# Second MLP product of a token tower from seven products of quarters

## The chip, the cores and the metric

The kernel runs on one core of one Trainium2 chip. The metric is the device time of one execution in microseconds; the time before is the median of three runs. A core has a matrix engine (TensorE, PE in the profile; PEld is its loading of weights), three engines for element-wise work (VectorE or DVE, ScalarE or ACT, GpSimd or POOL), an engine that here issues transfers (SyncE, SP), a working memory SBUF of 128 partitions, and the accumulator memory PSUM into which TensorE writes.

## The reference

A signal of shape (4, 64, 512, 64) is cut into patches, Fourier transformed and multiplied by a weight matrix: 16,384 tokens of 256 numbers. One layer follows: a retention block with an MLP, and a mixture of 8 experts of which each token takes 2. All in fp32. Cut to what matters here:

```python
# h: tokens [16384, 256]; x = layernorm(h)
hh = layernorm(x)
q, k, v = hh @ Wq.T + bq, hh @ Wk.T + bk, hh @ Wv.T + bv
mem_t = decay * mem_(t-1) + k_t * v_t          # scan along 4096 tokens
x = x + q * mem
h2 = layernorm(x)
mlp = relu(h2 @ W1.T + b1) @ W2.T + b2         # 256 -> 1024 -> 256
h = h + (x + mlp)
t = layernorm(h)                                # router and experts work on t
h = h + t + sum over two experts e of share_e * (gelu(t @ w1[e] + b1[e]) @ w2[e] + b2[e])
```

The change concerns the second product of the MLP, `relu(...) @ W2.T`: per block of 512 tokens a matrix of 512x1024 by one of 1024x256.

## The kernel before

32 blocks of 512 tokens (4 tiles of 128) go through a pipeline. In each period of the loop one block (`new`) is embedded, normalised and goes through retention, the block before it (`mid`) through the MLP, and the one before that (`old`) is routed: its rows are written to lists, one per expert, from which expert tiles of 256 rows are then taken. One such tile is worked off in a `slot`: `enter` (first expert product), `leave` (second product of the tile before), `sums` (results of that tile). The order of instructions on TensorE, VectorE and ACT is the order of the program text. The numbers D, KD, KH, TT, U are 256, 2, 8, 4 and 2.

```python
class Norm:
    def stats(self, src, t): ...              # bn_stats and bn_aggr on VectorE
    def factors_here(self): ...               # 1/sqrt(var + eps) on VectorE, 12 small operations
    def factors(self, twice=False): ...       # the same by pow on GpSimd
    def apply(self, dst, src, i=0):
        for t in range(TT):
            nc.vector.tensor_scalar(
                dst[:, t, :D], src[:, t, :], self.mv[:, t, 0:1],
                self.rstd[:, i, t : t + 1], ALU.subtract, ALU.mult)
...
    def residual(self):                       # block `new`, after retention
        norm = Norm()
        for u in range(U):
            ps = p_tm.tile([P, 2, D], F32, name="tm")
            for i in range(2):
                for k in range(KD):
                    nc.tensor.transpose(ps[:, i, ts(k, P)],
                        self.ret[:, k, ts(2 * u + i, P)], ident)
            nc.vector.tensor_tensor(self.z[:, ts(u, 2), :], ps, self.z[:, ts(u, 2), :], ALU.add)
            for i in range(2):
                norm.stats(self.z, 2 * u + i)
        norm.factors_here()
        self.zz = one.tile([P, TT, D], F32, name="zz")
        norm.apply(self.zz, self.z)
...
    def mlp_in(self, m):                      # aT: features x tokens, after the Relu
        ps = feature_mm(w1_sb, self.hT, m)    # two matmuls with 512 moving columns
        nc.scalar.activation(self.aT[:, m, :], ps, AF.Relu, bias=vec[:, MB1 + m : MB1 + m + 1])

    def mlp_out(self, u, between=None):
        if u == 0:
            self.norm = Norm()
        ps = p_tm.tile([P, 2, D], F32, name="tm")
        for i in range(2):
            ...
            for k in range(KH):
                nc.tensor.matmul(ps[:, i, :], lhsT=self.aT[:, k, ts(u * 2 + i, P)],
                    rhs=w2_sb[:, k, :], start=k == 0, stop=k == KH - 1)
        nc.vector.tensor_tensor(self.h[:, ts(u, 2), :], ps, self.h[:, ts(u, 2), :], ALU.add)
        for i in range(2):
            self.norm.stats(self.h, u * 2 + i)
        if u == U - 1:
            ...factors...
            self.tok = one.tile([P, TT, D], F32, name="tok")
            self.norm.apply(self.tok, self.h)
            ...
```

A period of the loop, with the engines that do most of each step:

```python
            next(embed)                # 40 matmul records of 256 columns, then stats, factors, apply
            ...
            slot(known)
            for m in range(KH):
                if mid: mid.mlp_in(m)
                if m == 1: new.split1()            # ACT; then a transposing DMA
                if m == TT - 1: slot(known)
                if m == KH - 3:
                    blocks[i + 1].differences(xs.pop(i + 1))
                    new.features1()                # hT from the DMA's result
            if old: ...logits...                   # router product
            for m in range(KD):
                new.retention(m)                   # 6 matmuls of 512 columns; kv, scan, ret on VectorE
                if old and m == 0: old.choose()
            if old: take(old.i + 1, old, old.place())
            slot(known)
            if mid: mid.mlp_out(0)
            new.residual()
            slot(known)
            ...
            new.split2()
            if mid: mid.mlp_out(1)
```

PSUM has three pools here: `p_mm` with four buffers, `p_tm` with three, `p_sm` with one[...].

Of the kernel before, what the change touches and what calls it, by code (L numbers as in the profile page):

```python
# [12 lines left out]
F32 = mybir.dt.float32  # L13
# [6 lines left out]
P = 128  # L20
# [15 lines left out]
def vit_tower_kernel(  # L36
# [20 lines left out]
    E = rw.shape[1]  # L57
    KD, KH = D // P, H // P
    J = STRIDE // 2
    TT = 4  # L60
# [88 lines left out]
    nc.sync.dma_start(out=w1_sb, in_=w1.rearrange("(k p) h -> p k h", p=P))  # L149
    w2_sb = const.tile([P, KH, D], F32)  # L150
    nc.sync.dma_start(out=w2_sb, in_=w2.rearrange("(k p) d -> p k d", p=P))
    rw_sb = const.tile([P, KD, E], F32)
# [62 lines left out]
    class Norm:  # L215
# [23 lines left out]
        def factors(self, twice=False):  # L239

            n = 2 if twice else 1
            self.rstd = small.tile([P, n, TT], F32, name=f"rstd{n}")
            nc.gpsimd.tensor_scalar(self.rstd[:, 0, :], self.mv[:, :, 1], EPS, None, ALU.add)  # L243
            if twice:
                nc.gpsimd.tensor_scalar(
                    self.rstd[:, 1, :], self.mv[:, :, 1], 1.0 + EPS, EPS * EPS, ALU.mult, ALU.add
                )
            nc.gpsimd.tensor_tensor(self.rstd, self.rstd, mhalf[:, 0:n, :], ALU.pow)

        def apply(self, dst, src, i=0):  # L250
# [58 lines left out]
    class Block:  # L309
# [32 lines left out]
        def embed(self):  # L342
# [38 lines left out]
            norm.factors(twice=True)  # L381
            yield
            self.z = one.tile([P, TT, D], F32, name="z")
            self.zz = one.tile([P, TT, D], F32, name="zz")
            norm.apply(self.zz, self.h, 1)
            norm.apply(self.z, self.h, 0)

# [57 lines left out]
        def residual(self):  # L445
            norm = Norm()
            for u in range(U):
# [7 lines left out]
                for i in range(2):  # L455
                    norm.stats(self.z, 2 * u + i)
            norm.factors_here()
            self.zz = one.tile([P, TT, D], F32, name="zz")
            norm.apply(self.zz, self.z)

# [4 lines left out]
        def split2(self):  # L465
            if self.i < EARLY:
                return
            self.turn = Turn()
            self.turn.split(self.zz)
# [8 lines left out]
        def mlp_in(self, m):  # L478
# [3 lines left out]
            nc.scalar.activation(self.aT[:, m, :], ps, AF.Relu, bias=vec[:, MB1 + m : MB1 + m + 1])  # L482

        def mlp_out(self, u, between=None):
            if u == 0:
                self.norm = Norm()
            ps = p_tm.tile([P, 2, D], F32, name="tm")
            for i in range(2):
                if i and between:
                    between()  # L490
                for k in range(KH):
                    nc.tensor.matmul(  # L492
                        ps[:, i, :],
                        lhsT=self.aT[:, k, ts(u * 2 + i, P)],
                        rhs=w2_sb[:, k, :],
                        start=k == 0,
                        stop=k == KH - 1,
                    )
            nc.vector.tensor_tensor(self.h[:, ts(u, 2), :], ps, self.h[:, ts(u, 2), :], ALU.add)
            for i in range(2):  # L500
                self.norm.stats(self.h, u * 2 + i)
            if u == U - 1:
                self.norm.factors_here() if self.i >= NS - 1 else self.norm.factors()
                self.tok = one.tile([P, TT, D], F32, name="tok")
                self.norm.apply(self.tok, self.h)
                if self.i == NS:
                    nc.vector.tensor_tensor(self.h, self.h, self.tok, ALU.add)
                    return
                mean, rstd = self.norm.mv[:, :, 0], self.norm.rstd[:, 0, :]
                self.by = small.tile([P, 2, TT], F32, name="by")  # L510
                nc.vector.tensor_scalar(self.by[:, 0, :], rstd, 1.0, None, ALU.add)
                nc.vector.scalar_tensor_tensor(self.by[:, 1, :], mean, -1.0, rstd, ALU.mult, ALU.mult)

        def store(self):

            by = self.by
            for t in range(TT):
                nc.scalar.activation(  # L518
                    self.h[:, t, :],
                    self.h[:, t, :],  # L520
                    AF.Identity,
                    bias=by[:, 1, t : t + 1],
                    scale=by[:, 0, t : t + 1],
                )

            self.stored = nc.sync.dma_start(out=rows_of(self.i), in_=self.h)
            unordered("sums", self.stored, ())

        def rows(self):

            self.row = two.tile([P, TT, RW], I32, name="row")
            for i, half in enumerate(halves(self.tok)):
# [154 lines left out]
    def take(n, block, writes):  # L687
# [24 lines left out]
        shape = [1, k, E]  # L712
        past = small.tile([1, KMAX, E], F32, name="past")[:, :k, :]
        nc.vector.tensor_tensor(
# [4 lines left out]
        )  # L719
        table_f = small.tile([1, 2, KMAX], F32, name="table_f")[:, :, :k]  # L720
        nc.vector.tensor_reduce(table_f[:, 0, :], past, AX.X, ALU.add)
# [214 lines left out]
    LEFT = 3  # L936

    def slot(known):

# [9 lines left out]
    with tc.manual_schedule(engines=MANUAL):  # L949
        blocks[0].differences(xs.pop(0))  # L950
        xs[1] = load_x(1)
        for i in range(NS):
# [14 lines left out]
            next(embed)  # L967
            next(embed)
            if mid:
                mid.sum_up()  # L970
            next(embed, None)
            slot(known)
# [4 lines left out]
            for m in range(KH):  # L977
                if mid:
                    mid.mlp_in(m)
                if m == 1:  # L980
                    new.split1()
                if m == TT - 1:
                    slot(known)
                if m == KH - 3:
                    blocks[i + 1].differences(xs.pop(i + 1))
                    new.features1()
            if i == NS - 1:
                slot(known)
            if old:
                for t in range(TT):  # L990
                    old.logits(t)
            for m in range(KD):
                new.retention(m)
                if old and m == 0:
                    old.choose()
            if old:
                take(old.i + 1, old, old.place())
            if i + 2 < NB:
                xs[i + 2] = load_x(i + 2)
            slot(known)  # L1000
            if mid:
                mid.mlp_out(0)
            new.residual()
            slot(known)
# [3 lines left out]
            if i == 0:  # L1008
                fold(w1_sb.unsqueeze(1), G2, B2, MB1)
            else:  # L1010
                new.split2()
            if mid:
                mid.mlp_out(1)

# [7 lines left out]
        next(embed)  # L1022
        next(embed)
        mid.sum_up()
        next(embed, None)
        expert_step()
        weights = load_bank()
        old.join3()
        for m in range(KH):
            mid.mlp_in(m)  # L1030
            if m in (1, 5):
                next(weights)
# [9 lines left out]
        writes = old.place()  # L1042
        next(weights)
        last.retention(0)
        mid.mlp_out(0)
        next(weights)
        take(NS - 1, old, writes)
        expert_step()
        mid.mlp_out(1)
        next(weights)  # L1050
# [21 lines left out]
        for m in range(KH):  # L1072
            last.mlp_in(m)
            if m == TT - 1:
                expert_step()
        expert_step()
        last.mlp_out(0, expert_step)
        expert_step()
        last.mlp_out(1, expert_step)

# [103 lines left out]
```

## Time and profile before

| | |
|---|---|
| median of three runs | 2202.25 us (2193.75 to 2203.81) |
| span of the profiled execution | 2216.1 us |
| busy: PE, DVE, ACT, POOL | 98%, 74%, 37%, 39% |
| second MLP product (L492) | 2048 matmul records of 256 columns |
| granted TensorE clock | 0.991 |

In a row of groups stand the line of the kernel, the engine, the operation, what it writes and reads, the shape and the count; after the first bar the busy time in us and the mean duration of one in ns; after the second the idle time of the engine ahead of these instructions, and what ended it. An fp32 matmul leaves two records, a transpose one. In a timeline the columns are start and length in us, then the group; idle time ahead of it stands in brackets.

### The profile page before, as it was taken

The numbers are of one execution on the slowest core, as the hardware profiler recorded it, in microseconds if no ns is written. First come the engines' busy times: TensorE is split into PE (matmuls) and PEld (weight loads), VectorE is DVE, ScalarE is ACT, GpSimd is POOL, SyncE is SP. The second block draws the span as 40 slices with busy tenths as digits, with TensorE's granted clock in tenths as the row PEclk, the third lists the DMA queues.
The fourth block names the chain that finished last, engine by engine and source line by source line (L and its number), as shares of the span: only waits on it lengthen the run. The fifth ranks groups of instructions, "written<-read, shape, count | busy, mean of one in ns | idle before, by whom it ended". The sixth has DMA issues, their size and how long they took to land.

```text
span 2216.1 us, 28920 instructions
## 1 busy us (share of the span) xinstructions
PE 2161.2 (98%) x8548; PEld 1544.3 (70%) x8548; DVE 1650.9 (74%) x5150; ACT 825.6 (37%) x1329; POOL 873.1 (39%) x760
## 2 busy tenths in 40 slices
PE   8999999999999999999999999999999999998999
PEld 6666666667676667777666777666677766676676
DVE  6678877778778777877877777777787777766454
ACT  1223323444334443432444432344443334442443
POOL 0022243344444434444434444443444444344444
PEclk9999999999999999999999999999999999999999
DMA  3022265676565677657567656665765666588743
GB/s 135 20 97 75 79 147 125 134 163 122 127 149 135 143 139 150 125 129 155 129 139 149 135 128 135 149 136 132 163 130 130 138 146 137 115 172 205 116 66 45
DMA packets 425389, 284.95 MB, mean 129 GB/s; under 512 B 355216, under 2 KB 391056, under 8 KB 421136
## 3 DMA queue, kind: packets, MB, share of 16 engines
q1 hardware_dynamic: 374304, 210.21, 41.4%
q0 software_dynamic: 49632, 67.39, 16.1%
q10 hardware_dynamic: 1296, 5.52, 1.0%
q8 instruction: 67, 1.10, 0.2%
q14 instruction: 90, 0.74, 0.1%
HBM read 118.36 MB, written 88.39 MB: 93 GB/s over the span
## 4 chain that ended last, share of the span: by engine, by line
PE 88%; DVE 3%; DMA 3%; ACT 3%; issue 2%; another core or an unknown queue 0%; POOL 0%; ACTq 0%; DVEq 0%; SPq 0%; POOLq 0%
PE mm L298 31%; PE tm L492 19%; PE tm L353 11%; PE mm L799 9%; PE tm L816 9%; DMA turned<-planes 3%; PE sm L557 2%; PE tm L888 1%; PE tm L451 1%; PE mm L871 1%; PE mm L131 1%; PE mm L265 1%; ACT h L518 1%; ACT row L533 1%; ACT hT L292 1%
## 5 line engine op out<-in xcount | busy, mean ns | idle before, releaser
L839 POOL DMA_INDIRECT out<-y,xg x262 | 429.3, 1638 | 501.0 <-DVE y L835 225.9
L492 PE MATMUL tm<-w_sb,aT 128*128 128x256 f32 x2048 | 462.3, 380 | 16.5 <-issue 14.6
L298 PE MATMUL mm<-hT,w_sb 128*128 128x512 f32 x1024 | 455.4, 596 | 10.7 <-ACT ge L807 5.7
L492 PEld LDWEIGHTS tm<-w_sb,aT 128*128 128x128 f32 x2048 | 387.2, 190 | 80.8 <-issue 27.1
L298 PEld LDWEIGHTS mm<-hT,w_sb 128*128 128x128 f32 x1024 | 193.9, 191 | 232.6 <-issue 207.6
L298 PE MATMUL mm<-hT,wqkv_sb 128*128 128x512 f32 x768 | 342.5, 602 | 4.2 <-DVE hT L292 4.2
L640 POOL DMA_INDIRECT xbuf<-row,to x248 | 242.3, 977 | 258.8 <-DVE full L699 182.4
L807 ACT ACTIVATE ge<-mm,w 128x256 f32<-128x256 f32 x262 | 109.3, 469 | 574.3 <-issue 525.8
L353 PE MATMUL tm<-wu,xv 128*128 128x256 f32 x1280 | 284.8, 381 | 0.0
L298 PEld LDWEIGHTS mm<-hT,wqkv_sb 128*128 128x128 f32 x768 | 145.3, 192 | 176.4 <-issue 160.4
L353 PEld LDWEIGHTS tm<-wu,xv 128*128 128x128 f32 x1280 | 244.3, 191 | 33.3
L799 PE MATMUL mm<-xT,w 128*128 128x256 f32 x1048 | 251.3, 383 | 1.5 <-DVE tile_share L828 1.5
L816 PE MATMUL tm<-w,ge 128*128 128x256 f32 x1048 | 247.6, 379 | 0.9 <-DVE y L833 0.9
L482 ACT ACTIVATE aT<-mm,vec 128x512 f32<-128x512 f32 x256 | 169.9, 684 | 173.7 <-PE mm L298 170.5
L799 PEld LDWEIGHTS mm<-xT,w 128*128 128x128 f32 x1048 | 195.6, 191 | 38.6 <-issue 13.1
L816 PEld LDWEIGHTS tm<-w,ge 128*128 128x128 f32 x1048 | 199.0, 190 | 31.3 <-issue 3.4
L792 ACT COPY xT<-xh 128x512 uint16<-128x512 uint16 x262 | 181.2, 761 | 5.4 <-DMA xh<-xbuf 5.3
L243 POOL TENSOR_SCALAR rstd<-mv 128x4 f32<-128x4 f32 x62 | 41.6, 671 | 319.2 <-DVE mv L224 317.3
L833 DVE TENSOR_TENSOR y<-tm,w 128x512 f32<-128x512 f32 x131 | 90.6, 692 | 70.5 <-PE tm L816 69.7
L416 ACT ACTIVATE ks<-mm,vec 128x512 f32<-128x512 f32 x64 | 44.0, 687 | 248.6 <-PE mm L298 248.6
L597 POOL TENSOR_TENSOR ex<-euler,second 128x4 f32<-128x4 f32 x32 | 34.7, 1084 | 247.1 <-DVE second L589 247.1
L418 DVE SCALAR_TENSOR_TENSOR kv<-mm,vec,ks 128x512 f32<-128x512 f32 x64 | 47.9, 748 | 108.9 <-PE mm L298 108.9
(155 smaller groups left out, 2498.2 us busy)
## 6 DMA issues: line engine op xcount, KB each, us to landing
w<-in_wex SPq DMA_DIRECT2D x113, 641.5 KB
xb<-in_x SPq DMA_DIRECT2D x32, 1040.0 KB
out<-h SPq DMA_DIRECT2D x31, 512.0 KB
bank<-in_wex ACTq DMA_DIRECT2D x8, 641.5 KB
out<-y,xg POOLq DMA_INDIRECT x262
xbuf<-row,to POOLq DMA_INDIRECT x248
xh<-xbuf SPq DMA_TRANSPOSE x131
xg<-xbuf SPq DMA_DIRECT2D x131, 4.0 KB
```

The lines of the kernel that those rows point to most:

```text
L298: nc.tensor.matmul(ps, lhsT=w[:, k, ts(m, P)], rhs=rhs[:, k, :], start=k == 0, stop=k == KD - 1)
L353: nc.tensor.matmul(ps[:, n, :], lhsT=xv[:, i, j, :], rhs=wu[:, i, j, :], start=j == 0, stop=j == J - 1)
L418: nc.vector.scalar_tensor_tensor(own_order(self.kv[:, m, :]), tiles_order(pv), vec[:, BV + m : BV + m + 1], own_order(ks), ALU.add, ALU.mult,)
L482: nc.scalar.activation(self.aT[:, m, :], ps, AF.Relu, bias=vec[:, MB1 + m : MB1 + m + 1])
L492: nc.tensor.matmul(ps[:, i, :], lhsT=self.aT[:, k, ts(u * 2 + i, P)], rhs=w2_sb[:, k, :], start=k == 0, stop=k == KH - 1,)
L640: write = nc.gpsimd.indirect_dma_start(out=xbuf, out_offset=bass.IndirectOffsetOnAxis(ap=to[:, c, t : t + 1], axis=0), in_=self.row[:, t, ...
L792: nc.scalar.copy(halves[:, :, :, 1 - i], self.xh[:, i * KD : (i + 1) * KD, :])
L799: nc.tensor.matmul(ps[:, m, :], lhsT=self.w[:, k * D + m * P : k * D + (m + 1) * P], rhs=self.xT[:, k, :], start=k == 0, stop=k == KD - 1,)
L807: nc.scalar.activation(self.ge[:, m, :], ps[:, m, :], AF.Gelu, bias=self.w[:, 5 * D + m : 5 * D + m + 1])
L816: nc.tensor.matmul(ps[:, c, :], lhsT=self.ge[:, k, ts(c, P)], rhs=w[:, (2 + k) * D : (3 + k) * D], start=k == 0, stop=k == KD - 1,)
L833: nc.vector.tensor_tensor(y, ps, w[:, 4 * D : 5 * D].unsqueeze(1).to_broadcast([P, 2, D]), ALU.add)
L839: add = nc.gpsimd.indirect_dma_start(out=out, out_offset=bass.IndirectOffsetOnAxis(ap=self.xg[:, c, NUMBER - D : NUMBER - D + 1], axis=0), ...
```

## The change

The product is split into quarters. With A the 512x1024 result of the Relu, split into A11, A12, A21, A22 (256 tokens by 512 features each), and B the weights, split into B11 to B22 (512 by 128), the kernel computes (Winograd's form of Strassen's method)

- S1 = A21 + A22, S2 = S1 - A11, S3 = A11 - A21, S4 = A12 - S2 for each block, on VectorE;
- T1 = B12 - B11, T2 = B22 - T1, T3 = B22 - B12, T4 = B21 - T2, once, on VectorE;
- M1 = A11 B11, M2 = A12 B21, M3 = S4 B22, M4 = A22 T4, M5 = S1 T1, M6 = S2 T2, M7 = S3 T3 on TensorE.

Seven products of quarters take the place of eight, for an eighth less arithmetic on the engine with the most busy time. (The signs of S3, T4 and the sums are arranged so that all results are added.) M1, M2 and M4 need no sum of quarters or only one of weights, and stand ahead of the residual of the next block; the other four stand where the second half stood. To make room on VectorE, ACT applies the layernorm factors (as scale and offset), GpSimd or VectorE computes the offset, and the choice of the next expert tiles (`take`) moves into the next period, between products of the MLP. Core of the diff, with cuts:

```diff
+        def apply_act(self, dst, src, i=0):
+            for t in range(TT):
+                nc.scalar.activation(dst[:, t, :D], src[:, t, :], AF.Identity,
+                    bias=self.less[:, i, t : t + 1], scale=self.rstd[:, i, t : t + 1])
...
+        def combine1(self):
+            self.A11, self.A12 = [self.aT[:, i * KQ : (i + 1) * KQ, : BLK // 2] for i in range(2)]
+            self.A21, self.A22 = [self.aT[:, i * KQ : (i + 1) * KQ, BLK // 2 :] for i in range(2)]
+            ...
+            nc.vector.tensor_tensor(self.S1, self.A21, self.A22, ALU.add)
+            nc.vector.tensor_tensor(self.S2, self.S1, self.A11, ALU.subtract)
+            nc.vector.tensor_tensor(self.S3, self.A11, self.A21, ALU.subtract)
+        def combine2(self, place):
+            self.S4 = one.tile([P, KQ, BLK // 2], F32, name=place)
+            nc.vector.tensor_tensor(self.S4, self.A12, self.S2, ALU.subtract)
         def mlp_out(self, u, between=None):
+            def product(to, a, b):
+                for i in range(2):
+                    for k in range(KQ):                      # KQ = 4
+                        nc.tensor.matmul(to[:, i, :], lhsT=a[:, k, ts(i, P)],
+                            rhs=w2_sb[:, b, k, :], start=k == 0, stop=k == KQ - 1)
+            def add(to, what):
+                nc.vector.tensor_tensor(to, to, what, ALU.add)
+            h = self.h.rearrange("p (a i) (c d) -> p a c i d", i=2, d=P)
+            U = self.aT[:, 0, : BLK // 2].rearrange("p (i d) -> p i d", d=P)
             if u == 0:
-                self.norm = Norm()
-            ...16 matmuls of 256 columns, add, stats...
+                self.ps = p_sm.tile([P, 2, 2, P], F32, name="sm")
+                product(self.ps[:, 0], self.A11, B11)                    # M1
+                nc.scalar.copy(U, self.ps[:, 0])
+                add(h[:, 0, 0], U)
+                return
+            if u == 1:
+                ps = p_tm.tile([P, 2, 2, P], F32, name="tm")
+                product(ps[:, 0], self.A12, B21)                         # M2
+                ...
+                product(ps[:, 1], self.A22, T4)                          # M4
+                add(h[:, :, 0], ps)
+                return
+            product(self.ps[:, 1], self.S2, T2)                          # M6
+            add(U, self.ps[:, 1])
+            add(h[:, 0, 1], U)
+            product(self.ps[:, 0], self.S1, T1)                          # M5
+            add(h[:, :, 1], self.ps[:, 0].unsqueeze(1).to_broadcast([P, 2, 2, P]))
+            ...
+            ps = p_tm.tile([P, 2, 2, P], F32, name="tm")
+            product(ps[:, 0], self.S3, T3)                               # M7
+            add(U, ps[:, 0])
+            add(h[:, 1], U.unsqueeze(1).to_broadcast([P, 2, 2, P]))
+            product(ps[:, 1], self.S4, B22)                              # M3
+            add(h[:, 0, 1], ps[:, 1])
+            self.norm = Norm()
+            for t in (2, 3, 0, 1):
+                self.norm.stats(self.h, t)
...
             for m in range(KH):
                 if mid: mid.mlp_in(m)
+                if m == 0: new.result1(1)             # layernorm result, by ACT
                 if m == 1:
                     new.split1()
+                    if 2 < i <= SOON:
+                        take(*placed)                 # of the period before
+                        known = len(tiles)
+                if m == 2: new.result1(0)
...
+            if mid: mid.combine1()
             for m in range(KD):
                 new.retention(m)
...
             if old:
-                take(old.i + 1, old, old.place())
+                placed = old.i + 1, old, old.place()
             slot(known)
             if mid:
                 mid.mlp_out(0)
+                mid.combine2("kv")
+                mid.mlp_out(1)
             new.residual()
             slot(known)
...
-            if mid: mid.mlp_out(1)
+            if mid: mid.mlp_out(2)
```

## The prediction

> **What bounds the kernel now.** I read the page's shares of busy time first, then the groups by form, then the timelines of TensorE and VectorE over one period of the main loop.
>
> ```profile
> PE 2161.2 (98%) x8548; PEld 1544.3 (70%) x8548; DVE 1650.9 (74%) x5150; ACT 825.6 (37%) x1329; POOL 873.1 (39%) x760
> PE 88%; DVE 3%; DMA 3%; ACT 3%; issue 2%; another core or an unknown queue 0%; POOL 0%; ACTq 0%; DVEq 0%; SPq 0%; POOLq 0%
> L492 PE MATMUL tm<-w_sb,aT 128*128 128x256 f32 x2048 | 462.3, 380 | 16.5 <-issue 14.6 <-DVE h L499 1.7
> L557 PE MATMUL sm<-rw_sb,tokT 128*128 128x8 f32 x512 | 59.4, 251 | 0.3 <-ACT tokT L266 0.2
> L451 PE MATMUL tm<-ident,ret 128*128 128x128 f32 x256 | 33.4, 273 | 1.5 <-DVE ret L436 1.5
> ```
>
> TensorE is the bound: 98% busy, 88% of the chain that ended last. A gain in TensorE work is worth its full time only if nothing new makes TensorE wait, because there is hardly any waiting now to absorb it.
>
> A matmul's own duration (380 ns) is no price here, since matmuls overlap. I price by the distance from start to start, from the timeline of TensorE over one period (start, length, group; the matmul records are two per fp32 matmul, one per transpose):
>
> ```profile
> 1011.50 10.54 PE L298 MATMUL mm<-hT,wqkv_sb 128*128 128x512 f32 x24 [0.79 <-DVE hT L292]
> 1021.87 0.53 PE L624 MATMUL sm<-both,rc 128*128 128x32 f32 x4
> 1022.23 1.97 PE L799 MATMUL mm<-xT,w 128*128 128x256 f32 x8
> 1024.04 1.89 PE L816 MATMUL tm<-w,ge 128*128 128x256 f32 x8
> 1025.77 7.07 PE L492 MATMUL tm<-w_sb,aT 128*128 128x256 f32 x32
> 1032.68 1.04 PE L451 MATMUL tm<-ident,ret 128*128 128x128 f32 x8
> 1033.55 1.89 PE L799 MATMUL mm<-xT,w 128*128 128x256 f32 x8
> 1035.28 1.89 PE L816 MATMUL tm<-w,ge 128*128 128x256 f32 x8
> 1037.01 7.27 PE L492 MATMUL tm<-w_sb,aT 128*128 128x256 f32 x32
> 1044.11 8.80 PE L353 MATMUL tm<-wu,xv 128*128 128x256 f32 x40
> ```
>
> From 1025.77 to 1032.68 are 32 records of 256 columns: 216 ns each. Transposes with 128 moving columns: 1032.68 to 1033.55, eight in 0.87 us, 109 ns each. The router product (8 moving columns, new weights for each) takes 112 ns a record in the trace (16 records, 1.79 us)[...]. One period, from the retention products at 1011.50 to the next at 1076.10, is 64.6 us; its records at these distances fill about 63.35, so all waiting in a period is about 1.25 us.
>
> VectorE in the same period, on the stretch that matters (residual, layernorm factors, the results of an expert tile):
>
> ```profile
> 1034.69 0.66 DVE L454 TENSOR_TENSOR z<-tm,z 128x512 f32<-128x512 f32 x1
> ...
> 1038.37 0.17 DVE L231 TENSOR_SCALAR mv<-mv 128x4 f32<-128x4 f32 x1
> ...
> 1041.09 1.38 DVE L252 TENSOR_SCALAR zz<-z,mv,rstd 128x256 f32<-128x256 f32 x4
> 1042.40 0.21 DVE L828 SCALAR_TENSOR_TENSOR tile_share<-xg,w 128x2 f32<-128x2 f32 x1
> ...
> 1043.48 0.62 DVE L835 TENSOR_SCALAR y<-y,tile_share 128x256 f32<-128x256 f32 x2
> 1044.31 0.69 DVE L499 TENSOR_TENSOR h<-tm,h 128x512 f32<-128x512 f32 x1 [0.22 <-PE tm L492]
> ```
>
> From the first residual add to the end of the factors VectorE needs 6.4 us without a pause (1034.69 to 1041.09), and 1.65 us for a tile's results (1042.40 to about 1044.05). It finishes barely before the second half of the MLP product does (it then waits 0.22 us). Nothing in the kernel before makes TensorE wait for this stretch: the 7.1 us of L492 at 1037.01 lie beside it.
>
> [...]
>
> **The change, part by part.**
>
> 1. Products. Before: 2 halves x 2 tiles x 8 = 32 matmuls of 256 columns, 64 records x 0.216 = 13.82 us a block. After: 7 products x 2 x 4 = 56 matmuls of 128 columns, 112 records. [...] I take 12.54: **-1.28 us** a block. The eighth of the arithmetic (1.73 us) isn't all kept.
>
> 2. Work of VectorE. Removed: four applications of the layernorm (4 x 1.31 to 1.38 = 5.4 us in sequence), two adds of 0.69, two small ones. Added: S1 to S4, each 128x1024 like L462 (1.19 to 1.23): 4.9 us; U and h additions, 5 of 256 elements (0.4) and 3 of 512 (0.69): 4.1 us. About +2 us on 50.6 busy of 64.6, so VectorE doesn't become the bound by its sum. ACT takes four groups like L518 (four in 2.07 us): +8.3 us, on 25.4 of 64.6 (the sum over the two stretches of one period). Also no bound.
>
> 3. S1, S2, S3 (3.65 us) stand ahead of the first `kv`. VectorE waited 3.26 us there for the projection, so they push the chain back by about 0.4 us; the first of the seven products must wait until the two PSUM reads of `place` are done, since it takes the only buffer of `p_sm`: **+0.2 us**.
>
> 4. M1, M2, M4 then run ahead of the residual; their additions don't hold TensorE. After the transposes and an expert slot come the other four, M6 (S2 T2), M5 (S1 T1), M7 (S3 T3), M3 (S4 B22). Here the built program has two new waits. M5's first matmul goes to the other half of M6's bank, and waits until VectorE has added M6 into U. M3's first goes to the other half of M7's bank, and waits for the addition of M7 into U. No other TensorE work stands between.
>
> 5. First wait. Count from the end of the first four transposes. TensorE: the other four 0.44, the slot 3.46, M6 16 x 0.112 = 1.79: done at 5.69. VectorE: about 0.4 to begin (end of the add of M2 and M4, matmul latency), 6.4 for residual and factors, 0.2 for the new offset, 1.65 for the slot's results, 0.42 for the add into U, 0.1 for the signal: 9.2. **+3.5 us** of idle TensorE.
>
> 6. Second wait. VectorE is free by then; TensorE waits for matmul end to start of the add (0.2: the last record of the first half of L492 gives way at 1032.68, and VectorE's add of it starts at 1032.88 in its timeline), the add (0.42) and the signal (0.1): **+0.7 us**.
>
> Sum of the stretch from retention to the next embedding: -1.28 + 0.2 + 3.5 + 0.7 = +3.1; about 0.3 of waiting that is there now (32.61 us against 32.27 of records) is swallowed: +2.8.
>
> 7. From the embedding to the retention: results by ACT take 2.07 instead of 1.31 and GpSimd has a further operation, but ACT starts without waiting for VectorE, `take` no longer stands ahead of the slot, and the split for the second turn begins earlier. The 0.9 us of waiting there (0.74 for ACT, 0.79 for hT) may shrink or grow a little: -0.2, an estimate.
>
> So **+2.6 us** a period. Expert tiles run in the last 25 of the 31 blocks of the loop with a slot between: 25 x 2.6 = 65 us. In the five before with an MLP (about 52 us long) there is no slot between the transposes and M6: TensorE is through at 2.23, VectorE at 7.5, a wait of 5.3; 5.3 + 0.7 - 1.28 - 0.5 swallowed = 4.2, x 5 = 21 us. Beginning and end I take as unchanged. 2202 + 86 = **2288 us**.
>
> **Rivals.** (a) TensorE doesn't wait: then only part 1 counts, 31 x 1.28 to 1.6 = 40 to 50 us less, 2152 to 2162. For it: TensorE is the bound, and three products were moved ahead. Against: the two waits are in the program, and 8.8 us of VectorE work can't lie beside 5.7 of TensorE. (b) The waits stay, but what they delay is repaid: ACT and the turn by DMA get time, and the waits of now vanish. At most 1.25 us a period come back: 2202 + 25 x 1.5 + 15 = 2255. (c) The rows of 128 columns go slower than 112 ns[...]: at 120 ns the gain falls to 0.4 and the time rises by a further 25 us. (d) ACT, now with four groups more between the Relus, holds the four `mm` buffers, or the turn comes later and the 0.79 us ahead of the retention grow: 1 us a period, +25. I hold the first two additions of waiting for certain and (c), (d) for small.
>
> **Range and chances.** From (b), 2255, to (c) or (d) on top of the sum, 2313: eight times in ten 2252 to 2318. Under 2158, only (a) holds: 0.04. Within 2% (2158 to 2246), if half the wait is absent: 0.09. Slower by over 2%: 0.87.
>
> **What would show it.** Records of the new products 112 ns apart inside a product; TensorE idle before M5 about 3.5 us and before M3 about 0.7 us a period, released by the adds into U; periods of about 67 us for 64.6; idle VectorE before `kv` gone; no change in the bounds by sum. If M5 starts right behind M6, or VectorE gets to its add into U before M6 ends, I am wrong. If the records stand 120 apart, part 1 is wrong.

## The result, and the profile after

| | before | after |
|---|---|---|
| median of 4 runs, us | 2203.03 (2193.75 to 2207.95) | 2460.98 (2456.75 to 2463.76) |
| ratio, 95% interval | 1 | 1.1175 [1.1133, 1.1217] |
| mean granted clock of TensorE, profiled run | 0.991 | 0.947 |
| one steady period (embedding to embedding), mean of 20, us | 65.1 | 71.65 |

The change costs 258 us. The prediction said 86: the direction was right, the size was not. The two profiled executions are 246 us apart: 131 us lie in 20 steady periods (6.5 each), 64 in the five ahead of them, 46 in the last five, where the wait for the add is 4.9 to 6.2 us.

The page and the waits of TensorE in the changed kernel (engine with tile and line, what it waited for, us in total, times, longest). Line 554 holds the matmuls of the seven products, line 563 their additions on VectorE, line 729 VectorE's second read of the choice:

```profile
PE 2215.0 (90%) x10084; PEld 1640.5 (67%) x10084; DVE 1724.0 (70%) x5004; ACT 1082.7 (44%) x1865; POOL 938.0 (38%) x852
L554 PE MATMUL sm<-w_sb,tok 128*128 128x128 f32 x512 | 118.7, 425 | 166.0 <-DVE aT L563 161.3
...
L554 PE MATMUL tm<-w_sb,aT 128*128 128x128 f32 x1536 | 204.0, 295 | 0.0
```

```profile
PE sm L554 <- DVE aT L563: 161.3, 31, 6.2
PE tm L554 <- DVE aT L563: 16.9, 32, 1.0
PE mm L332 <- ACT aT L529: 11.0, 8, 2.4
PE sm L554 <- DVE before L729: 10.2, 3, 3.5
```

TensorE, 98% busy before, is 90% busy. The first line is M5 waiting for the addition of M6 into U: 161.3 us in 31 blocks, 5.2 each (5.64 on average in the steady periods, 4.6 to 4.7 in the early ones). The second is M3 waiting for the addition of M7: 0.53 each. The group `sm<-w_sb,tok` is M5 alone, and the bar after its busy time gives 425 ns for a record of it, 295 ns for one of M2, M4 and M7 (`tm<-w_sb,aT`), which have the same shape. The idle time has a column of its own there: the waits aren't all.

One steady period, TensorE (start, length, group, idle time ahead):

```profile
1159.46 2.02 PE L554 MATMUL sm<-w_sb,aT 128*128 128x128 f32 x16
1161.32 3.74 PE L554 MATMUL tm<-w_sb,aT 128*128 128x128 f32 x32
1164.89 1.04 PE L491 MATMUL tm<-ident,ret 128*128 128x128 f32 x8
1165.76 1.89 PE L898 MATMUL mm<-xT,w 128*128 128x256 f32 x8
1167.49 1.89 PE L915 MATMUL tm<-w,ge 128*128 128x256 f32 x8
1169.22 1.95 PE L554 MATMUL sm<-w_sb,tokT 128*128 128x128 f32 x16
1176.96 3.78 PE L554 MATMUL sm<-w_sb,tok 128*128 128x128 f32 x16 [5.79 <-DVE aT L563]
1180.54 2.50 PE L554 MATMUL tm<-w_sb,aT 128*128 128x128 f32 x16
1183.55 2.05 PE L554 MATMUL tm<-w_sb,kv 128*128 128x128 f32 x16 [0.52 <-DVE aT L563]
1185.44 8.80 PE L387 MATMUL tm<-wu,xv 128*128 128x256 f32 x40
```

In order: M1; M2 and M4; transposes; slot; M6; the first wait; M5; M7; the second wait; M3; the next embedding. M6 takes 1.95 us for its 16 records (eight matmuls), M5 3.78 for as many. The view by windows shows why (window, its length, busy time and count of TensorE, of its weight loads, VectorE, ACT and GpSimd, then the granted clock, DMA share, GB/s):

```profile
1171.20:1174.80 3.60, 0.00 (x0) 0.00 (x0) 2.57 (x10) 2.67 (x5) 2.93 (x3) 1.00 0.26 77
1174.80:1176.90 2.10, 0.00 (x0) 0.00 (x0) 0.42 (x1) 1.39 (x2) 1.39 (x2) 0.52 0.62 70
1176.90:1181.70 4.80, 4.74 (x22) 4.74 (x23) 1.12 (x3) 0.00 (x0) 2.28 (x2) 0.50 0.92 140
1181.70:1185.30 3.60, 3.08 (x27) 2.90 (x27) 1.11 (x2) 0.00 (x0) 0.82 (x1) 1.00 0.49 61
```

TensorE stands still from 1171.17; 3.69 us later, from 1174.86 to 1181.69, its granted clock is halved (6.83 us, twice 3.41), and M5 and a third of M7 run in that time. A period so costs 1.83 us more in M5 (3.78 for 1.95) and 0.55 in M7 (2.50 for 1.95): 2.4 us that stand in no list of waits. All 20 steady periods have these 6.83 us, beginning 3.35 to 4.53 us after M6's end. In the whole run the clock is halved for 262 us, for 40 us in the kernel before.

VectorE just ahead of the second start of TensorE:

```profile
1171.90 0.16 DVE L268 SCALAR_TENSOR_TENSOR less<-mv,rstd 128x4 f32<-128x4 f32 x1
...
1172.35 0.69 DVE L932 TENSOR_TENSOR y<-tm,w 128x512 f32<-128x512 f32 x1
1173.08 0.90 DVE L934 TENSOR_SCALAR y<-y,tile_share 128x256 f32<-128x256 f32 x2
1176.48 0.42 DVE L563 TENSOR_TENSOR aT<-aT,sm 128x256 f32<-128x256 f32 x1 [2.51 <-remote]
1176.94 0.42 DVE L563 TENSOR_TENSOR h<-h,aT 128x256 f32<-128x256 f32 x1
```

The chain that step 5 counted ends here at 1173.98, as it should: from then a wait of about 3.3 us would have been left. But the add into U begins only at 1176.48. It waits on one semaphore, TensorE's for M6, and the trace records that update at 1176.46, though M6's last record ended at 1171.17. TensorE's report comes 5.3 us late, and VectorE stands still for 2.5 us. It is so in all 20 steady periods (the add starts 5.1 to 5.3 us behind M6's end, VectorE stands still for 2.3 to 2.5). Nothing in the prediction had this.

### The profile page after: what moved, and what is told of

The parts are those of the page before. It is cut to its first block, busy times and chain, and to the rows that moved or that the text cites. A ratio compares the mean times of both kernels' runs of the same rounds, so it can differ in the third digit from the quotient of the medians.

```text
span 2462.0 us, 32721 instructions
## 1 busy us (share of the span) xinstructions
PE 2215.0 (90%) x10084; PEld 1640.5 (67%) x10084; DVE 1724.0 (70%) x5004; ACT 1082.7 (44%) x1865; POOL 938.0 (38%) x852
## 5 line engine op out<-in xcount | busy, mean ns | idle before, releaser
L938 POOL DMA_INDIRECT out<-y,xg x262 | 434.5, 1658 | 379.2 <-DMA out<-y,xg 82.2
L739 POOL DMA_INDIRECT xbuf<-row,to x248 | 263.3, 1062 | 258.2 <-DVE tile_share L930 139.2
L554 PE MATMUL sm<-w_sb,tok 128*128 128x128 f32 x512 | 118.7, 425 | 166.0 <-DVE aT L563 161.3
L554 PEld LDWEIGHTS sm<-w_sb,tok 128*128 128x128 f32 x512 | 109.6, 325 | 172.1 <-DVE aT L563 167.2
L554 PE MATMUL tm<-w_sb,aT 128*128 128x128 f32 x1536 | 204.0, 295 | 0.0
L554 PEld LDWEIGHTS tm<-w_sb,aT 128*128 128x128 f32 x1536 | 201.8, 214 | 0.1
L256 POOL TENSOR_SCALAR rstd<-mv 128x4 f32<-128x4 f32 x62 | 14.1, 228 | 483.0 <-DVE mv L237 483.0
L396 ACT COPY ab<-tm 128x512 f32<-128x512 f32 x32 | 18.8, 586 | 366.4 <-PE tm L387 366.4
```

What stands on the lines that cost most here:

```text
L554: nc.tensor.matmul(to[:, i, :], lhsT=a[:, k, ts(i, P)], rhs=w2_sb[:, b, k, :], start=k == 0, stop=k == KQ - 1,)
L739: write = nc.gpsimd.indirect_dma_start(out=xbuf, out_offset=bass.IndirectOffsetOnAxis(ap=to[:, c, t : t + 1], axis=0), in_=self.row[:, t, ...
L938: add = nc.gpsimd.indirect_dma_start(out=out, out_offset=bass.IndirectOffsetOnAxis(ap=self.xg[:, c, NUMBER - D : NUMBER - D + 1], axis=0), ...
```

## The experiments

"Before" was run beside each (2198.55 to 2210.84 us in the batches); each ratio has its 95% interval.

### Is it the two waits?

**banks.** M5 and M7 share a bank (one buffer of a PSUM pool, here of `p_tm`) of their own, M3 has another, and no matmul waits for an addition:

```diff
-            product(self.ps[:, 0], self.S1, T1)
-            add(h[:, :, 1], self.ps[:, 0]...)
-            ps = p_tm.tile([P, 2, 2, P], F32, name="tm")
-            product(ps[:, 0], self.S3, T3)
-            add(U, ps[:, 0])
+            ps = p_tm.tile([P, 2, 2, P], F32, name="tm")
+            product(ps[:, 0], self.S1, T1)
+            product(ps[:, 1], self.S3, T3)
+            add(h[:, :, 1], ps[:, 0]...)
+            add(U, ps[:, 1])
             add(h[:, 1], U...)
+            ps = p_tm.tile([P, 2, 2, P], F32, name="tm")
             product(ps[:, 1], self.S4, B22)
```

> M5 and M7 share a bank of their own, M3 has another, and the additions of M5 and M7 come after both, so TensorE waits for no addition. Theory (the two waits and the halved clock that follows them are the whole loss): periods fall from 71.7 us to 63 to 64.5, 2165 to 2205 us in all, and the granted clock is back at 0.99. Rival (the added work on VectorE and ACT, or slower products of 128 columns, is the loss): stays above 2350 us.

Measured: 2257.21 us, ratio 1.0263 [1.0231, 1.0295]. Some 204 us of the 258 are gone with the two waits (and the halved clock behind them), but the run stays above the 2165 to 2205 expected. Its waits:

```profile
PE mm L332 <- DVE hT L326: 26.4, 20, 2.7
PE sm L554 <- DVE before L730: 10.5, 4, 3.5
```

TensorE now waits ahead of the retention for the turned hT: once it is no longer late, the way from the embedding over ACT's results and the turn is. The clock is still halved for 131 us.

**addfirst.** The waits stay, but the slot's results (`y`) come behind the add of M6:

```diff
-            slot(known)
+            slot(known, sums=False)
 ...
-                mid.mlp_out(2)
+                mid.mlp_out(2, late=lambda: advance("sums", at["leave"]))   # behind add(U, M6)
```

> VectorE adds M6 into U ahead of the results of the expert tile of that slot, instead of after them. Theory (the first wait is VectorE's program order): the wait falls from 5.8 to about 1.2 to 1.7 us (VectorE done with the residual and factors at 7.0 of the count, TensorE at 5.7)[...], 2260 to 2310 us. Rival (something other than order holds the add at the end of the turn's split on ACT or of GpSimd's transfers, 2.3 us after VectorE is free): the add still starts 4.4 us after the offset, no gain, 2440 to 2465 us.

Measured: 2306.66 us, ratio 1.0481 [1.045, 1.0513]. The wait for the add falls to 66.5 us in 32 blocks: 1.3 us in a steady period, as the theory had it, 4.6 in the early ones and 2.9 in the last five. The clock is not halved once between 393 and 1755 us, and the steady period is 64.64 us, no longer than in the kernel before.

```profile
1168.86 2.05 PE L554 MATMUL sm<-w_sb,tok 128*128 128x128 f32 x16 [1.31 <-DVE aT L563]
```

What is left of the loss lies in the first four periods with an MLP (60 to 68 us for 52), the one behind them (74 for 64) and the last five (68 to 72 for 64 to 65).

### Is it the clock?

**filler.** Six matmuls of 512 columns between M6 and M5, their result not used; the wait is kept:

```diff
             add(h[:, 0, 1], U)
+            if self.i < NS - 1:
+                filler = p_mm.tile([P, BLK], F32, name="mm")
+                for _ in range(6):
+                    nc.tensor.matmul(filler, lhsT=ident, rhs=w1_sb[:, 0, :BLK], start=True, stop=True)
             product(self.ps[:, 0], self.S1, T1)
```

> Six matmuls of 512 columns (5.15 us) with a result that nobody reads stand between M6 and M5; the wait on VectorE stays. Theory (the idle of 5.8 us halves the clock for two windows of 3.4 us, in which M5 takes 3.6 us instead of 1.8): M5 starts as late as before but M5 to M3 run at full clock, about 2.4 us less a period, 2375 to 2400 us. Rival (the waiting alone counts): 2455 to 2470 us or slower.

Measured: 2368.55 us, ratio 1.077 [1.0736, 1.0803]: more work, and 92 us less than the changed kernel. The clock stays full from 346 to 2189 us, and M5 takes 1.95 us again. TensorE (M6, the six matmuls, M5, M7), then VectorE:

```profile
1123.37 1.95 PE L554 MATMUL sm<-w_sb,tokT 128*128 128x128 f32 x16
1125.15 5.32 PE L588 MATMUL mm<-w_sb,ident 128*128 128x512 f32 x12
1130.30 1.95 PE L554 MATMUL sm<-w_sb,tok 128*128 128x128 f32 x16
1132.09 1.95 PE L554 MATMUL tm<-w_sb,aT 128*128 128x128 f32 x16
```

```profile
1127.24 0.89 DVE L938 TENSOR_SCALAR y<-y,tile_share 128x256 f32<-128x256 f32 x2
1128.05 0.41 DVE L563 TENSOR_TENSOR aT<-aT,sm 128x256 f32<-128x256 f32 x1
```

M5 starts 4.98 us behind M6's end, not 5.64 or 5.79, so a steady period (68.22 us, 3.4 less) owes some 0.6 us to that and 2.4 to the clock: the halved clock is a cost of its own. The add of M6 isn't late here: it follows `y` without a gap in every steady period.

### What holds up the report of M6?

**noiota.** GpSimd's iota, which ends just ahead of the late add, is replaced by an addition of a constant on VectorE.

```diff
-            nc.gpsimd.iota(self.row[:, :, NUMBER : NUMBER + 1], pattern=[[1, TT]], base=self.i * BLK, ...)
+            nc.vector.tensor_scalar(self.row[:, :, NUMBER], numbers_f, float(self.i * BLK), None, ALU.add)
```

> The changed kernel, but the row numbers of a block are written by VectorE (one addition of a constant, 128x4) and not by GpSimd's iota, which stands right ahead of the end of the held-up add of M6 into U. Theory A (something in GpSimd's chain at that place, its iota behind the indirect transfer, holds VectorE's add back by 2.3 us): the add follows VectorE's results of the expert tile directly, the wait ahead of M5 falls from 5.8 to about 3.5 us[...], and the total falls to 2340 to 2420 us. Theory B (the hold-up has to do with TensorE's standing idle or with ACT, not with the iota): wait and time as in the changed kernel, about 2455 us.

Measured: 2445.24 us, ratio 1.1065 [1.1038, 1.1092]. The add still comes 0.9 to 2.4 us after VectorE's results in the 20 steady periods (2.3 to 2.5 in the changed kernel), and the total is 16 us lower: the iota is not what holds it up.

**noadd.** The two indirect additions to the output of the slot ahead of M6 are left out, so those results are missing:

```diff
             new.residual()
-            slot(known)
+            slot(known, write=False)       # sums() without its indirect_dma_start
```

> The changed kernel, but GpSimd leaves out the two indirect additions to the output of the expert tile whose slot stands between the transposes and M6 (those results are missing from the output). In the changed kernel the semaphore with which TensorE reports M6 is recorded only at 1176.46, 5.3 us after M6's last record and 0.45 us after the second of these transfers has been issued. Theory A (TensorE's report is held up while GpSimd issues indirect transfers): with the two gone, the report comes soon after the last of the eight scatters, some 3 us earlier; the add into U follows VectorE's results directly, the wait ahead of M5 falls from 5.8 to 3.3 to 3.6 us, the clock is halved less, and the time falls to 2290 to 2390 us. Theory B (the late report has another cause, TensorE standing still or ACT's copies): 5.8 us and about 2450 us.

Measured: 2462.93 us, ratio 1.1146 [1.1118, 1.1174], the report at 1176.34. No difference, and the expectation had misread the trace: the two transfers that GpSimd issues at 1172.5 and 1174.5 are still there. They are those of the slot ahead, behind the scatters on GpSimd; the ones left out would have come later.

**latescatter.** Nothing is left out; the eight scatters of a block's rows are handed to GpSimd behind the slot:

```diff
             if old:
                 placed = old.i + 1, old, old.place()      # place() without its scatters
 ...
             new.residual()
             slot(known)
+            if old and not old.writes:
+                old.scatter()
             if mid:
                 mid.mlp_out(2)
```

> The changed kernel with the eight indirect scatters of a block's rows issued behind the slot ahead of M6, not ahead of the residual; nothing is left out. Theory A (GpSimd's indirect transfers hold up TensorE's report of M6): GpSimd is then idle when the slot's results are ready, its two additions are issued at once and the scatters collide with M6 to M3 instead; the report is late in another way, the wait stays between 3.5 and 6 us, 2380 to 2480 us. Theory B (only a full queue of transfers, eight scatters and then two additions, holds it up): the wait falls to 3.5 us or less, 2290 to 2390 us, unless the layernorm factors of the next block, which stand behind the scatters on GpSimd, come later and cost as much.

Measured: 2390.58 us, ratio 1.0823 [1.0798, 1.0848], 70 us less than the changed kernel. TensorE and then VectorE (M6, M5, M7; the results, the add):

```profile
1133.31 1.95 PE L554 MATMUL sm<-w_sb,tokT 128*128 128x128 f32 x16
1138.35 2.71 PE L554 MATMUL sm<-w_sb,tok 128*128 128x128 f32 x16 [3.10 <-DVE aT L563]
1140.86 2.96 PE L554 MATMUL tm<-w_sb,aT 128*128 128x128 f32 x16
```

```profile
1136.45 0.69 DVE L937 TENSOR_TENSOR y<-tm,w 128x512 f32<-128x512 f32 x1
1137.17 0.80 DVE L939 TENSOR_SCALAR y<-y,tile_share 128x256 f32<-128x256 f32 x2
1137.89 0.41 DVE L563 TENSOR_TENSOR aT<-aT,sm 128x256 f32<-128x256 f32 x1
```

The report of M6 is recorded at 1135.27, where M6 ends; the add follows `y` without a gap; the wait is 3.10 us. It is so in every steady period; in the last five, reports come 1 to 4.6 us late again. In this kernel GpSimd issues three scatters, two result transfers and five scatters in that stretch; in the changed one eight scatters and then two result transfers, each transfer 0.3 us behind the one before:

```profile
1161.52 1.07 POOL L739 DMA_INDIRECT xbuf<-row,to  x1 [6.43 <-DVE tile_share L930]
...
1174.45 1.56 POOL L938 DMA_INDIRECT out<-y,xg  x1 [0.30 <-issue]
```

The run is as long in both (14.6 and 14.5 us); its order has changed. That the report comes in time with another order, and that in the changed kernel it comes 0.2 to 0.4 us behind the end of the run in all 20 steady periods, ties it to these transfers. But they are not enough: `filler` has the same eight and two (1115.67 to 1130.36), with M6's report at 1125.33 for a last record that ends at 1125.32, and in `addfirst` the add starts 0.8 us behind M6's end in the midst of such a run. Fetches of instructions, a further rival, fall elsewhere in each period (here at 1162.3 and 1168.5). What else is needed, and how the report is held up, the runs don't show.

### Is it the rest of the change?

**rest.** The second product as before, all else of the change kept:

```diff
-            product(self.ps[:, 0], self.A11, B11)       # and the other six, with S1 to S4
+            for k in range(KH):
+                nc.tensor.matmul(ps[:, i, :], lhsT=self.aT[:, k, ts(u * 2 + i, P)], rhs=w2_sb[:, k, :], ...)
 ...
-            mid.combine1() ... combine2("kv") ... combine_weights()
```

> All other parts of the change (layernorm results by ACT, offset by GpSimd, choice of tiles a period later), with the second MLP product as it was: 32 matmuls of 256 columns, no sums of quarters. Theory: these parts cost nothing, 2185 to 2215 us. Rival (ACT or the later choice of tiles is part of the loss): 2240 us or more.

Measured: 2329.42 us, ratio 1.0601 [1.0559, 1.0643]: the theory missed by over 110 us, and the rival held. TensorE waits 49.5 us for hT and 21.4 for an expert tile's Gelu, both ACT's line of work: zz begins 18.5 us after the embedding, for 16.2 in the two kernels compared, since ACT still has the block before's copies, its `tok`, its row and its store to do.

**rest_zz** gives zz back to VectorE:

```diff
-                self.norm1.apply_act(self.zz, self.h, 1)
+                self.norm1.apply(self.zz, self.h, 1)
```

> The run 'rest' (second product as before, all else of the change), with one more thing undone: the first layernorm result zz of a block is applied by VectorE again, not by ACT behind hT, tok, row and the store. Theory A (the late zz lengthens the way from the embedding to the turned hT, for which TensorE then waits with 'rest'): zz begins about 16 us after the embedding for 18.5, the waits for hT (49.5 us) go back to a few us, 2190 to 2220 us. Theory B (something else in the rest costs the time, such as the expert tiles being taken a period later): over 2290 us.

Measured: 2336.37 us, ratio 1.0593 [1.0564, 1.0622]. No gain: zz begins still later, at 23 us, because it now stands on VectorE behind the turned rows of the block before, which ACT delivers late. So it isn't zz alone. As it looks, the seven products' waits hide a slow ACT chain in the changed kernel, and versions without them meet it.

Against rest, banks is 72 us faster: with the rest of the change in both, the seven products in banks of their own gain, and more than the 40 us of step 1 (31 blocks of 1.28); why more is open. What costs is the shared banks and the rest of the change. The seven products in banks of their own with everything else as in the kernel before were not run.

### M1 and the early periods

The changed kernel in an early period, where no slot stands between the choice and M1:

```profile
228.75 0.53 PE L723 MATMUL sm<-both,rc 128*128 128x32 f32 x4
232.75 3.65 PE L554 MATMUL sm<-w_sb,aT 128*128 128x128 f32 x16 [3.47 <-DVE before L729]
...
247.28 3.78 PE L554 MATMUL sm<-w_sb,tok 128*128 128x128 f32 x16 [4.64 <-DVE aT L563]
```

M1 waits 3.47 us for the one small PSUM buffer and then runs at half the clock (0.50 from 232.78 to 236.19; 3.65 us for 2.02 in the steady period), like M5 later.

**order** puts M2 and M4 ahead of M1:

```diff
-                mid.mlp_out(0)
-                mid.combine2("kv")
                 mid.mlp_out(1)
+                mid.mlp_out(0)
+                mid.combine2("kv")
```

> The changed kernel with M2 and M4 ahead of M1. Theory A (in periods without a slot M1 waits for VectorE's reads of the choice): the waits of 3.5 us ahead of M1 in three early periods (10.2 us) and the halved clock behind them go, the first five periods with an MLP shrink from 60 to 68 us to 56 to 62, the steady ones stay at 71.6: 2425 to 2450 us. Theory B (these early waits are hidden behind others): within 5 us of the changed kernel.

Measured: 2459.03 us, ratio 1.1146 [1.1114, 1.1177]. The waits of M1 are gone and the first four periods with an MLP go from 60 to 68 us to about 63, but the total is the same within its interval: what was gained there is lost in longer waits for the add.

### Are these all?

**banks_zz** is banks with the edit of rest_zz, **banks_zz_order** that with the edit of order too, and **banks_order** banks with the edit of order alone:

> The run 'banks' (seven products whose additions TensorE doesn't wait for) with zz applied by VectorE as before the change. Theory A (with the waits gone, the way embedding, zz by ACT, turn, hT bounds): 2140 to 2190 us, waits for hT well under the 26 us of 'banks', periods 63 to 64 us. Theory B (VectorE, which gets 1.3 us of work back in its fullest stretch, then bounds): 2230 to 2270 us.

> The same with M2 and M4 ahead of M1, so that M1, which needs the one small PSUM buffer, doesn't stand idle for VectorE's read of the last choice in periods without an expert slot. Theory A: the waits ahead of M1 (10 us in all) and the halved clock behind them go, 15 to 20 us less than the run with M1 first: 2130 to 2175 us. Theory B (they overlap with other waits of these early periods): less than 5 us.

> The run 'banks' (no wait of TensorE for an addition) with M2 and M4 ahead of M1, the results of the layernorm by ACT as in the changed kernel. Theory A: only the early periods gain, as in 'order': 2225 to 2250 us. Theory B (as in the runs with zz on VectorE, the head start that TensorE loses by waiting less shows up elsewhere, as stops inside a product while its reports are late): 2270 us or more.

Measured: 2277.05 (1.0316 [1.0294, 1.0338]), 2366.72 (1.0707 [1.068, 1.0734]) and 2305.22 us (1.0443 [1.0414, 1.0472]): each slower than banks, where each Theory A had it faster. The middle one shows it best, TensorE and then ACT:

```profile
1246.74 1.95 PE L555 MATMUL sm<-w_sb,tokT 128*128 128x128 f32 x16
1249.30 0.27 PE L555 MATMUL tm<-w_sb,tok 128*128 128x128 f32 x1 [0.61 <-issue]
1250.03 0.27 PE L555 MATMUL tm<-w_sb,tok 128*128 128x128 f32 x1 [0.46 <-issue]
1251.43 0.27 PE L555 MATMUL tm<-w_sb,tok 128*128 128x128 f32 x1 [1.14 <-issue]
1252.84 0.60 PE L555 MATMUL tm<-w_sb,tok 128*128 128x128 f32 x2 [1.14 <-issue]
1253.59 2.69 PE L555 MATMUL tm<-w_sb,tok 128*128 128x128 f32 x11
```

```profile
1243.93 1.39 ACT L893 COPY xT<-xh 128x512 uint16<-128x512 uint16 x2
1253.68 0.84 ACT L908 ACTIVATE ge<-mm,w 128x256 f32<-128x256 f32 x2 [8.36 <-issue]
```

M5 here has nothing to wait for, and yet its records come up to 1.4 us apart; ACT meanwhile waits 8.4 us for a product that TensorE finished at about 1245. Both go on together at 1253.6, when GpSimd's transfers are out (the last issue ends at 1253.0). It looks like the late report again, and this time TensorE itself stops. The Gelu of the same slot is 6.7 us late in the kernel before too (it starts at 1042.13 for matmuls that end at 1035.44; TensorE's update is recorded at 1042.06), but there nothing on the path wants it.

**banks_late, banks_order_late, banks_zz_order_late**: the scatters of latescatter on top.

> The run 'banks' (no wait of TensorE for an addition) with the scatters of 'latescatter' on top. Theory A (the late reports cost nothing once TensorE doesn't wait for the additions; what is left there is the wait for hT): within 15 us of the 2257 us of 'banks'. Theory B (they cost in 'banks' too): 2200 to 2240 us.

> The run 'banks_order' (2305 us: no wait for additions, M2 and M4 ahead of M1) with the scatters of 'latescatter' on top. Theory A (the stops inside M5 there, 61.6 us with halved clock behind them, come of TensorE's reports being held up, so that they go with the burst of transfers): 2190 to 2245 us, steady periods of 64 to 65 us and early ones of 51 to 53. Theory B (the stops have another cause): within 15 us of 2305 us.

> The same with zz applied by VectorE again ('banks_zz_order' was at 2367 us, with 67 us of stops inside M5). Theory A (stops gone; the way from the embedding over zz to hT as short as with ACT): 2170 to 2240 us, steady periods of 63.3 to 64.6 us. Theory B (VectorE, then the fullest engine but TensorE, or the turned rows of the block before, which it waits for ahead of zz, bound): 2260 us or more.

Measured: 2235.88 (1.016 [1.0124, 1.0196]), 2231.49 (1.013 [1.0098, 1.0162]) and 2255.73 us (1.025 [1.021, 1.0291]), that is 21, 74 and 111 us less than without. The stops inside M5 are gone from the two that had them (61.6 us in banks_order, 67.1 in banks_zz_order), as the theory of the late report has it. banks had none, and no late report of M6 either, so that its 21 us are not explained by it. In banks_order_late the first four periods with an MLP are 52.5 to 52.8 us, those of the kernel before; three steady ones without a halved clock take 62.9 to 63.1 us, for a median of 64.9 in the kernel before. Of the 258 us 33 are left, none of the versions beats the kernel before, and giving zz to VectorE makes it worse.

**keep1, keep2** try whether these 33 are the clock alone: it is halved there in the retention, behind the router product and a wait for hT.

```profile
1018.63 1.85 PE L657 MATMUL sm<-rw_sb,tokT 128*128 128x8 f32 x16
1021.12 12.23 PE L332 MATMUL mm<-hT,wqkv_sb 128*128 128x512 f32 x24 [0.64 <-DVE hT L326]
```

(banks_order_late: 12.23 us for the retention, 10.54 at full clock.) One matmul of 512 columns, or two, with a result not used, stand between the two lines:

> The run 'banks_order_late' (2231 us) with one 512-column matmul (0.86 us) between the router product and the retention, its result not used. Theory A (the halved clock in the retention comes of the idle stretch there): most of it goes, periods of 63 to 64 us, 2190 to 2220 us. Theory B (the wait for hT itself is the cost): 2231 to 2245 us.

> The same with two such matmuls (1.72 us). Theory A: the clock stays full in nearly all periods, but the second matmul lies partly beside no wait, 2195 to 2225 us. Theory B: 2245 to 2260 us.

Measured: 2306.39 (1.045 [1.0398, 1.0503]) and 2283.9 us (1.0334 [1.0298, 1.037]). Both theories missed. The clock was halved for 132 and 81 us (131 in banks_order_late), but zz now begins 18.5 us after the embedding, for 16.4, and some stops inside the products are back (11 us in keep1), though the scatters stand late. What the last 33 us are stays open; that they sit where TensorE waits for hT (28.8 us in banks_order_late) is seen, what would remove them is not.

## Why the prediction was wrong

Step by step, for a steady period (+6.5 us on average; the prediction had +2.6):

- **Step 1, products, held.** M6's records and those of the other products at full clock stand 112 ns apart, as the router product's of 8 columns do in the kernel before: 12.54 us for the 112 records of a block, where the 64 before took 13.82, the -1.28 of the prediction. The three periods of banks_order_late with the clock full are 1.8 us shorter than the median before, with about as much waiting in them (0.7 us for 0.9).
- **Step 2 held**: VectorE and ACT, at 70% and 44%, don't bound by their sums. It did miss that ACT's order of work becomes a chain: rest shows it, the changed kernel hides it (hT waits of 2.2 us in all).
- **Step 3, +0.2**, held where a slot stands ahead of M1. In three early periods it is 3.5 us and a halved clock.
- **Step 4 held**: both waits exist (161.3 and 16.9 us), and are what banks removes; TensorE has no record in the first one (1171.20 to 1176.90), not of M7 either, which stands behind M5. The waits are the program's; no run shows what the shared banks would do without them.
- **Step 5, the first wait, +3.5, is the step that failed.** It measured 5.79 in the period shown, 5.64 on average. The count of VectorE's work was right: latescatter, with the report in time, waits 3.10. Its two estimates measured 0.36 for 0.4 (the beginning: from the fifth transpose at 1165.33 to the add of z at 1165.69) and 0.06 for 0.1 (the signal: the add into U ends at 1176.90, M5 starts at 1176.96). But step 5 let VectorE add as soon as it was free, at about 8.7 of its count, and took for granted that TensorE, done with M6 at 5.69, had reported by then. The report came 5.3 us after M6, which holds the add back by 2.5.
- **Step 6, +0.7**, measured 0.52.
- **A term that the sum didn't have**, as large as the error of step 5: the clock, +2.4 us a period.
- **Step 7, -0.2**, can't be told apart in the changed kernel; embedding to retention is 30.98 us for 31.9, but because TensorE comes late to it and finds all ready.

Of the steady period: 2.6 predicted, +2.1 for the longer first wait, -0.2 for the shorter second, +2.4 for the clock give 6.9, for 6.5 measured; 0.4 is left over. The five early blocks were to cost 4.2 us each; the four periods before the first slot grew by 8.8 (the first) and by 13.7 to 15.9, for M1's wait, a wait of 2.3 us for ACT's Relu, M5's wait of 4.64 (predicted: 5.3) and the halved clock behind each. The last five periods, which the prediction counted as steady, grew by 7 to 11 us; no run takes these apart. Of the rivals none held; (a), no wait, was refuted in the first view, and (c) by the 112 ns.

The range had 2318 as its upper end because all its rivals priced the idle time at its own length. Here TensorE idle for 6.3 us a period cost 8.7.

## What to carry to other kernels

A stretch in which TensorE stands still is to be priced at its length plus the halved clock behind it (2.4 us behind 5.6 to 5.8 here); waits of 1.3 us were free of that (addfirst), while waits of 2.9 and 3.1 us were not (addfirst, latescatter), nor most of those of 0.6 us behind the router product (banks_order_late). Where a matmul waits, as M5 did here for 5.2 us a block, for another engine's read of the half bank beside it, give it a bank of its own first: banks took back 204 of the 258 us. And ask of a new wait on TensorE's result how long its report takes in that stretch (5.3 us here), not only when the matmul ends; a late report that nobody waited for in the old order becomes a cost in the new one.

## What was not expected of the hardware

- TensorE's semaphore update for a finished product came 5.3 us after its last record while GpSimd issued eight scatters and two indirect additions back to back. With another order of the ten (`latescatter`), or with the same ten and TensorE at work behind M6 (`filler`), it came within 0.01 us in the periods shown. In banks_zz_order TensorE's own matmuls stopped too, up to 1.4 us a record.
- The halved clock comes in stretches of 3.41, 6.83 or 10.24 us in the changed kernel (all but one that the run's end cuts off), and the idle time ahead of one can be shorter than 3.41: in latescatter 3.10 us of it (1135.26 to 1138.35) were followed by a halved clock from 1139.56 to 1142.97, 1.2 us after matmuls had begun again; in banks_order_late a wait of 0.64 us behind the router product, whose matmuls move 8 columns, was followed by 3.41 us of halved clock from 1022.41 (in three other steady periods waits of 0.66 us at this place were not). In addfirst waits of 1.3 us had no halved clock behind them. What decides it, the runs don't show.
